# Moving the compressed entries' causal mask from TensorE to VectorE, both heads at once, and reordering the start of an attention kernel

## The chip, the core and the metric

The kernel runs on one core of a Trainium2 chip. The metric is device time in microseconds; a kernel's time is the median of its runs. The core has a matrix engine (TensorE, PE in the profile; its weight loads are PEld), VectorE (DVE), ScalarE (ACT), GpSimd (POOL) and SyncE (SP), which here only issues DMAs. PE writes to PSUM; the other data lies in SBUF.

## What is computed

Four sequences of 1024 tokens with 512 features go through one block. With `xn` the layer-normalized input, the output is `x + attn(xn) + ffn(xn)`, where `ffn` is one product with operands rounded to 8-bit floats. The attention has 16 heads of 128 and two branches that share queries:

```python
q = apply_rope(rmsnorm(q, qn_w), pos)
entries = jnp.einsum('bcr,bcrh->bch', w_cmp, hidden_states.reshape(Bq, C, RATIO, HID))
ck = apply_rope(rmsnorm(entries @ Wk + bk, kn_w), block_ends)
sc = jnp.einsum('bhsd,bcd->bhsc', q, ck) * scale
sc = jnp.where(causal, sc, NEG)
tv, ti = jax.lax.top_k(sc, TOPK)
...
sl = jnp.einsum('bhcqd,bhckd->bhcqk', qc, kw) * scale
sl = jnp.where(mask[None, None], sl, NEG)
pl = jax.nn.softmax(sl, axis=-1)
...
merged = (ctx_sparse + ctx_local) * 0.5
```

Four tokens make one compressed entry. A token weighs the 8 best entries whose block has ended, with a softmax over those 8, and separately the tokens of its own and the previous window of 128. Both contexts are averaged and go through `Wo`.

## The kernel before

The work is cut into chunks of 128 tokens (8 per sequence, 32 in all) and each chunk into 8 units of two heads, so there are 256 units. All weights stay in SBUF. One Python loop (lines 835 to 904) writes the program out; each engine runs its instructions in that order. Its step `s` mixes stages of several units, so that a unit is spread over six steps:

- `queries` of unit s+3 (L478): queries and window keys of two heads, four products of 512 columns. In chunk 0 a bias product (L486) follows; later chunks have the bias folded into the weights by `fold_first_row` (L269), which chunk 0 runs once per unit.
- `squares` (L318, ScalarE) and `spread` (GpSimd) of s+3 give the RMS norm; `normalize` of s+2 (L506, VectorE) applies it and starts `rotate`: a GpSimd product (L332), a VectorE product (L333), and behind a `yield` two VectorE combinations (L335, L336), run later by `end_rotation`.
- Keys and queries must be transposed. In chunk 0 PE does it (`turn_keys_here`, L534) and `keep_keys` copies them out (L540 ScalarE, L541 VectorE). Later `turn_keys` of s+2 transposes 32x32 blocks on VectorE (L556, L559), stores them to DRAM (L564) and `fetch_keys` loads them back in the other order (L574), all from SP's queue.
- `scores` of s, for each head: previous window (L616), own window (L623), entries (L626), and a product of an identity and the mask in bf16 (L627) that adds the causal mask to the last 32 entries. Each head has a PSUM tile `sc` of one bank.
- `weigh` of s, for each head: add the window's mask and take the smallest negated score (L649), the 8 largest entries (L652), their negated maximum (L654), mark the 8 (L655, into `taken`), and two exponentials on ScalarE (L656, L664).
- `settle` of s, for each head: multiply by the marks and sum (L671), floor and reciprocal of the two sums (L680, L681), scale the entries (L682); `settle_window` scales the window on ScalarE (L687).
- `turn` of s transposes blocks of the probabilities (L705), stores them (L713), and `fetch` loads them (L747). In chunk 0 and the last unit `turn_here` (L728) uses PE, and `keep_turned` copies (L736) one head on ScalarE and one on VectorE.
- `values_of` of s+1 (L581) and `keep_values` (L593); `values` of s-1 (L764) makes the context, `keep_context` of s-2 (L779) copies it and `to_output` of s-2 (L797) multiplies by `Wo`.

Two generators run beside this by `steps()`: `chunk_prep` (layer norm, entries, their keys and values) and `chunk_eight` (the 8-bit product). For chunk 0 `until` runs `chunk_prep` up to named steps before the loop and in its first three steps. The PSUM tag `pp` has two buffers, shared in turn by xp, yp, tq, vp, tp and others.

At the start, loads are issued from SP's and ScalarE's queues in program order. A queue's issue can wait until an earlier load has landed: eight DMA semaphores are used in turn, and an issue that reuses one waits for its former load.

Of the kernel before, what the change touches and what calls it, by code (L numbers as in the profile page):

```python
# [38 lines left out]
def kernel(  # L39
# [93 lines left out]
    load_x(0, "norm")  # L133
    load_wqk(0, nc.sync)
    load_x(1, "norm")
    load_angles(0)

    wkv_sb = const.tile([P, KK, 2 * D + 1], F32, name="wkv_sb")
    nc.sync.dma_start(wkv_sb[:, :, 0:D], Wk.rearrange("(k p) n -> p k n", p=P))
    nc.sync.dma_start(wkv_sb[:, :, D : 2 * D], Wv.rearrange("(k p) n -> p k n", p=P))  # L140
    load_wlv(0, nc.sync)
    load_wqk(1, nc.sync)
    load_angles(1)
    load_wlv(1, nc.sync)
    load_wqk(2, nc.sync)
    load_wlv(2, nc.sync)


    with nc.allow_non_contiguous_dma(reason="512 words once"):
        nc.scalar.dma_start(  # L150
            wkv_sb[:, :, 2 * D : 2 * D + 1], Wcmp.rearrange("(k p) o -> p k o", p=P)
        )
    bias_f = work.tile([P, 1024], F32, tag="probT", name="bias_f", bufs=1)[0:BLK, 0:512]
    nc.vector.memset(bias_f, 0.0)
    nc.scalar.dma_start(bias_f[0:NU, 0:256], bq.rearrange("(u n) -> u n", u=NU))
    nc.scalar.dma_start(bias_f[0:NU, 256:512], blk.rearrange("(u n) -> u n", u=NU))
    bkv_sb = const.tile([NE, 2 * D], F32, name="bkv_sb")
    nc.scalar.dma_start(bkv_sb[:, 0:D], bk.partition_broadcast(NE))
    nc.scalar.dma_start(bkv_sb[:, D : 2 * D], bv.partition_broadcast(NE))
    norm_w = const.tile([P, 2, D], F32, name="norm_w")  # L160
    nc.scalar.dma_start(norm_w[:, 0, :], qn_w.partition_broadcast(P))
    nc.scalar.dma_start(norm_w[:, 1, :], kn_w.partition_broadcast(P))
    blv_n = work.tile([P, 2, P], F32, tag="cT", name="blv_n", bufs=1)[0:NH, 0, :]
    nc.scalar.dma_start(blv_n, blv.rearrange("(h d) -> h d", h=NH))
    bcmp_sb = const.tile([P, 1], F32, name="bcmp_sb")
    nc.scalar.dma_start(bcmp_sb, bcmp.partition_broadcast(P))
    scales = const.tile([P, 2], F32, name="scales")
    nc.scalar.dma_start(scales[:, 0:1], scale.partition_broadcast(P))
    nc.scalar.dma_start(scales[:, 1:2], scale1.partition_broadcast(P))


    nhalf = const.tile([P, 4], F32, name="nhalf")
# [7 lines left out]
    ident_b = const.tile([P, P], BF16, name="ident_b")  # L180
    inv = const.tile([P, 1], F32, name="inv")
    bias_b = const.tile([P, 512], BF16, name="bias_b")
    nc.vector.memset(bias_b, 0.0)
# [136 lines left out]
    def rotate(th, cs, nh, a, name):  # L320

        p = th.shape[0]
        a = a.rearrange("p (h t f) -> p h t f", h=nh, t=2)
        bb = work.tile([p, nh, 2, HALF], F32, tag=f"ropeb{nh}", name=f"rb_{name}", bufs=1)
        x12 = th[:, :, 0:ROPE].rearrange("p h (t f) -> p h t f", t=2)

        def wide(v):
            return v.unsqueeze(1).unsqueeze(1).to_broadcast([p, nh, 2, HALF])  # L330

        nc.gpsimd.tensor_tensor(bb, x12, wide(cs[:, HALF:ROPE]), ALU.mult)  # L332
        nc.vector.tensor_tensor(a, x12, wide(cs[:, 0:HALF]), ALU.mult)  # L333
        yield
        nc.vector.tensor_tensor(x12[:, :, 0, :], a[:, :, 0, :], bb[:, :, 1, :], ALU.subtract)  # L335
        nc.vector.tensor_tensor(x12[:, :, 1, :], a[:, :, 1, :], bb[:, :, 0, :], ALU.add)  # L336
# [5 lines left out]
    def chunk_prep(t):  # L342
# [14 lines left out]
        if c == 0:  # L357
            nc.gpsimd.memset(cv, 0.0)
        yield "B0"

        off = work.tile([P, 2], F32, tag="off", name=f"off_{t}")
        nc.gpsimd.tensor_scalar(off[:, 0:1], st[:, 6:7], -1.0, None, ALU.mult)
        nc.scalar.activation(
            xt, xt, AF.Identity, bias=off[:, 0:1], scale=1.0, accum_out=off[:, 1:2]
        )
        nc.gpsimd.tensor_scalar(off[:, 1:2], off[:, 1:2], 1.0 / HID, None, ALU.mult)
        yield "A1"
        xn = scratch(f"xn_{t}")
        nc.vector.tensor_scalar(xn, xt, off[:, 1:2], r, ALU.subtract, ALU.mult)
# [149 lines left out]

    def end_rotation(n):  # L520
        for _ in units[n].pop("rotation"):
            pass
# [13 lines left out]
    def keep_keys(n):  # L536
        w = units[n]
        tq = w.pop("tq").rearrange("p (t g a i) -> p t g a i", t=2, g=2, a=NB)
        qT, lkT = key_tiles(n)
        nc.scalar.copy(qT.rearrange("p a (i g) -> p g a i", g=2), tq[:, 0])  # L540
        nc.vector.tensor_copy(lkT.rearrange("p a (g i) -> p g a i", g=2), tq[:, 1])  # L541
# [55 lines left out]
    heads = {}  # L597
# [9 lines left out]
    def scores(n, h):  # L607
        t, _ = place(n)
        c, m, loc, spa = columns(n)
        w = units[n]  # L610
        qT, lkT = w["qT"], w["lkT"]
        ckT, _ = entries[t // NCH]
        sc = psum.tile([P, 512], F32, tag="sc", name=f"sc_{n}_{h}")
        q = qT[:, :, h]
        if c:
            nc.tensor.matmul(  # L616
                blocks(sc[:, 0:P]),
                q,
                units[n - NU]["lkT"][:, :, ds(h * BLK, BLK)],
                start=True,  # L620
                stop=True,
            )
        nc.tensor.matmul(  # L623
            blocks(sc[:, P : 2 * P]), q, lkT[:, :, ds(h * BLK, BLK)], start=True, stop=True
        )
        nc.tensor.matmul(sc[:, spa], q, ckT[:, 0:m], start=True, stop=False)  # L626
        nc.tensor.matmul(  # L627
            sc[:, ds(2 * P + m - NE, NE)],
            ident_b,
            mask_b[:, 2 * P : 2 * P + NE],  # L630
            start=False,
            stop=True,
        )
        heads[n, h] = {"sc": sc}

    def weigh(n, h):
        c, m, loc, spa = columns(n)
        w = heads[n, h]
        sc = w.pop("sc")
        top = work.tile([P, 8], F32, tag="top", name=f"top_{n}_{h}")  # L640
        neg = work.tile([P, 2], F32, tag="neg", name=f"neg_{n}_{h}")
        tot = work.tile([P, 2], F32, tag="tot", name=f"tot_{n}_{h}", bufs=3)
        taken = work.tile([P, 2 * P], BF16, tag="taken", name=f"taken_{n}_{h}")
        prob = probs[h]
        if n % (NU * NCH) == 0:

            nc.gpsimd.memset(prob[:, 2 * P + NE : 4 * P], 0.0)

        nc.vector.tensor_tensor_reduce(  # L649
            sc[:, loc], sc[:, loc], mask_b[:, loc], -1.0, TAKEN, ALU.add, ALU.min, neg[:, 0:1]  # L650
        )
        nc.vector.max(top, sc[:, spa])  # L652

        nc.vector.tensor_scalar(neg[:, 1:2], top[:, 0:1], -1.0, 1e29, ALU.mult, ALU.min)  # L654
        nc.vector.match_replace(taken[:, 0:m], top, sc[:, spa], TAKEN)  # L655
        nc.scalar.activation(  # L656
            prob[:, loc],
            sc[:, loc],
            AF.Exp,
            bias=neg[:, 0:1],  # L660
            scale=-1.0,
            accum_out=tot[:, 0:1],
        )
        nc.scalar.activation(prob[:, spa], sc[:, spa], AF.Exp, bias=neg[:, 1:2])  # L664
        w.update(tot=tot, taken=taken, prob=prob)

    def settle(n, h):
        c, m, loc, spa = columns(n)
        w = heads[n, h]
        tot, taken, prob = w["tot"], w["taken"], w["prob"]  # L670
        nc.vector.scalar_tensor_tensor(  # L671
            prob[:, spa],
            taken[:, 0:m],
            TAKEN_FROM,
            prob[:, spa],
            ALU.is_ge,
            ALU.mult,
            accum_out=tot[:, 1:2],
        )
        nc.vector.tensor_scalar(tot, tot, 1e-9, None, ALU.max)  # L680
        nc.vector.reciprocal(tot, tot)  # L681
        nc.vector.tensor_scalar(prob[:, spa], prob[:, spa], tot[:, 1:2], None, ALU.mult)  # L682

    def settle_window(n, h):
        _, _, loc, _ = columns(n)
        prob, tot = heads[n, h]["prob"], heads[n, h]["tot"]
        nc.scalar.mul(prob[:, loc], prob[:, loc], tot[:, 0:1])  # L687
# [10 lines left out]
    def turn(n):  # L698
# [4 lines left out]
        for h in range(2):  # L703
            prob = heads.pop((n, h))["prob"]
# [11 lines left out]
    def turn_here(n):  # L716
# [4 lines left out]
        for h in range(2):  # L721
            prob = heads.pop((n, h))["prob"]
# [8 lines left out]
    def keep_turned(n):  # L731
# [3 lines left out]
        for h, tp in enumerate(w.pop("tp")):  # L735
            (nc.vector.tensor_copy if h else nc.scalar.copy)(  # L736
# [89 lines left out]

    first, rounding = chunk_prep(0), round_w2()
    until(first, "A1")
    nc.vector.tensor_copy(ident_b, ident)
# [5 lines left out]
    for s in range(-3, NN + 2):  # L835
# [13 lines left out]
        for_unit(s, (weigh, 0), (weigh, 1))  # L849
        for_unit(s + 3, (queries,))  # L850
        if s + 1 < NU:
            for_unit(s + 1, (turn_keys_here,))
        for_unit(s, (settle, 0), (settle, 1))
        for_unit(s, (settle_window, 0), (settle_window, 1))
        for_unit(s + 2, (normalize,))
        if by_dma(s):
            turn(s)
        if s < 0:
            until(first, ("B3", "B4", "B6")[s + 3])
# [7 lines left out]
        if s + 2 >= NU:  # L867
            for_unit(s + 2, (turn_keys,))
        if s == -1:
            until(first, "B7")  # L870
        for_unit(s + 1, (values_of,))
# [15 lines left out]
        if s < NU:  # L887

            if s == -1:
# [61 lines left out]
```

## Time and profile before

| | us |
|---|---|
| median of 3 runs (2798.2 to 2800.68) | 2800.16 |
| the profiled execution | 2798.32 |
| its span | 2796.6 |
| to the first scores | 44.2 |
| chunk 0's eight units | 113.6 |
| the other 248 units | 2616.4 |
| from the last unit's scores to the end | 22.4 |

The mean granted TensorE clock over the span is 0.994; over the first 44.2 us it is 0.92, over chunk 0 0.89, and in between up to the last unit 1.00.

In a row of the profile, `L627 PE MATMUL sc<-mask_b,ident_b` is line, engine, operation and output from inputs; `xN` counts instructions, "mean ns" is the mean of one, and "idle before" the time its engine stood idle just ahead of them, with what ended it. In rows of a time line the first number is the start, the second the time up to the end of the last of the merged instructions. A product in fp32 appears as two instructions. In rows of waits the three numbers are the sum, the count and the longest.

### The profile page before, as it was taken

What the parts mean: (1) busy time and instruction counts of PE and PEld (TensorE: products, weight loads), DVE (VectorE), ACT (ScalarE), POOL (GpSimd) and SP (SyncE); (2) the same over time, 40 slices, a digit from 0 to 9 for tenths busy, and PEclk for the clock granted to TensorE, in tenths of its full rate; (3) what the DMA queues carried; (4) which work ended last, traced back from release to release, by engine and by line L of the source; (5) the groups of instructions that cost most, each with busy time, mean ns of one, the idle gap of its engine ahead of it and who ended that gap; (6) DMA issues with size and microseconds to landing.
All of it is one profiled execution on the core that took longest, in us unless ns stands there. A gap on an engine that the chain in (4) does not pass through costs nothing.

```text
span 2796.6 us, 48466 instructions
## 1 busy us (share of the span) xinstructions
PE 2735.4 (98%) x12721; PEld 1856.4 (66%) x12721; DVE 2263.3 (81%) x9171; ACT 1345.1 (48%) x5170; POOL 842.6 (30%) x1225
## 2 busy tenths in 40 slices
PE   5799999999999999999999999999999999999998
PEld 3566666676666666666666666666666666666765
DVE  4687888888877788888888787888888878888886
ACT  2345544445455554444445455454444545544443
POOL 2333332233332333322233322333223333222321
PEclk9899999999999999999999999999999999999999
DMA  6345445555544545555554454555555444455554
GB/s 203 98 119 139 136 136 155 154 154 154 146 125 139 139 141 141 154 152 152 153 142 134 132 140 138 152 155 145 153 149 143 129 139 139 136 152 161 145 150 125
DMA packets 623187, 401.96 MB, mean 144 GB/s; under 512 B 307152, under 2 KB 576320, under 8 KB 622912
## 3 DMA queue, kind: packets, MB, share of 16 engines
q1 hardware_dynamic: 610688, 385.29, 50.2%
q10 hardware_dynamic: 12224, 13.56, 1.6%
q8 instruction: 104, 1.70, 0.3%
q14 instruction: 171, 1.40, 0.2%
HBM read 214.64 MB, written 184.03 MB: 143 GB/s over the span
## 4 chain that ended last, share of the span: by engine, by line
PE 92%; DVE 2%; DMA 1%; issue 0%; SPq 0%; ACT 0%; POOL 0%; DVEq 0%; ACTq 0%; POOLq 0%
PE qp L478 30%; PE op L797 15%; PE vp L581 15%; PE cp L764 14%; PE sc L626 5%; PE sc L616 4%; PE sc L623 4%; PE yp L386 2%; PE fp L458 1%; PE ep L416 1%; PE xp L373 0%; DVE wqk L269 0%; DMA probT<-pr 0%; PE sc L627 0%; DVE th L506 0%
## 5 line engine op out<-in xcount | busy, mean ns | idle before, releaser
L478 PE MATMUL qp<-wqk,xnT 128*128 128x512 f32 x2048 | 944.7, 604 | 2.8 <-issue 2.1
L332 POOL TENSOR_TENSOR rb<-th,cs 128x256 f32<-128x256 f32 x256 | 248.1, 969 | 1673.7 <-DVE th L506 1673.7
L478 PEld LDWEIGHTS qp<-wqk,xnT 128*128 128x128 f32 x2048 | 370.3, 191 | 382.9 <-issue 371.7
L581 PEld LDWEIGHTS vp<-wlv,xnT 128*128 128x128 f32 x2048 | 393.0, 192 | 181.6 <-issue 115.8
L581 PE MATMUL vp<-wlv,xnT 128*128 128x256 f32 x2048 | 490.9, 383 | 17.9 <-DVE lkT L541 13.6
L656 ACT ACTIVATE prob<-sc,neg 128x256 f32<-128x256 f32 (+1 forms) x512 | 235.6, 460 | 550.9 <-DVE taken L655 540.4
L797 PE MATMUL op<-wo,cT 128*128 128x512 f32 x1024 | 488.0, 599 | 0.5 <-ACT cT L779 0.5
L649 DVE CUSTOM_DVE_ANT_0 sc<-sc,mask_b 128x256 f32<-128x256 f32 (+1 forms) x512 | 208.0, 406 | 279.8 <-PE sc L627 279.6
L593 ACT COPY lv<-vp 128x256 f32<-128x256 f32 x256 | 95.2, 372 | 471.6 <-PE cp L764 412.7
L687 ACT ACTIVATE prob<-prob,tot 128x256 f32<-128x256 f32 (+1 forms) x512 | 252.4, 493 | 129.1 <-DVE tot L681 127.8
L797 PEld LDWEIGHTS op<-wo,cT 128*128 128x128 f32 x1024 | 186.4, 190 | 189.4 <-issue 129.2
L764 PE MATMUL cp<-probT,lv 128*128 128x128 f32 x1920 | 300.7, 277 | 6.3 <-DMA probT<-pr 5.7
L318 ACT ACTIVATE junk<-qp 128x128 bf16<-128x128 f32 x1024 | 279.7, 273 | 33.1 <-PE qp L478 5.0
L506 DVE SCALAR_TENSOR_TENSOR th<-qp,r,norm_w 128x128 f32<-128x128 f32 x1024 | 286.8, 343 | 5.7 <-ACT junk L318 3.2
L764 PEld LDWEIGHTS cp<-probT,lv 128*128 128x128 f32 x1920 | 275.5, 193 | 23.4 <-issue 10.3
L705 DVE STREAM_TRANSPOSE probB<-prob 128x512 f32<-128x512 f32 (+2 forms) x494 | 281.9, 608 | 0.0
L313 POOL TENSOR_TENSOR r<-r,nhalf 128x4 f32<-128x4 f32 x256 | 260.5, 1018 | 21.3
L764 PE MATMUL cp<-probT,cv 128*128 128x128 f32 x1536 | 257.1, 277 | 0.0
L626 PE MATMUL sc<-ckT,qT 128*128 128x96 f32 (+7 forms) x1024 | 226.3, 303 | 0.0
L764 PEld LDWEIGHTS cp<-probT,cv 128*128 128x128 f32 x1536 | 214.8, 194 | 0.0
L623 PE MATMUL sc<-lkT,qT 128*128 128x128 f32 x1024 | 207.9, 285 | 0.0
L779 ACT ACTIVATE cT<-cp,blvT 128x128 f32<-128x128 f32 x512 | 160.0, 364 | 92.7 <-PE cp L764 83.4
(130 smaller groups left out, 3802.1 us busy)
## 6 DMA issues: line engine op xcount, KB each, us to landing
pr<-probB SPq DMA_DIRECT2D x127, 512.0 KB, 2.6
probT<-pr SPq DMA_DIRECT2D x508, 128.0 KB, 2.9
qk<-thb SPq DMA_DIRECT2D x992, 64.0 KB, 1.8
pr<-probB SPq DMA_DIRECT2D x96, 384.0 KB, 2.3
probT<-pr SPq DMA_DIRECT2D x384, 96.0 KB, 2.4
qT<-qk SPq DMA_DIRECT2D x248, 128.0 KB, 2.9
lkT<-qk SPq DMA_DIRECT2D x248, 128.0 KB, 2.8
x_norm<-_attn_hidden_states_dram SPq DMA_DIRECT2D x32, 256.0 KB, 3.0
```

Source lines behind the costliest of these rows:

```text
L313: nc.gpsimd.tensor_tensor(r, r, nhalf[: ss.shape[0], 0:n], ALU.pow)
L318: nc.scalar.activation(junk[: src.shape[0]], src, AF.Square, accum_out=acc)
L332: nc.gpsimd.tensor_tensor(bb, x12, wide(cs[:, HALF:ROPE]), ALU.mult)
L478: nc.tensor.matmul(qp, xnT[:, k if k or not t else KK, :], wqk_sb[u][:, k, :], start=(k == 0), stop=(t > 0 and k == KK - 1),)
L506: nc.vector.scalar_tensor_tensor(th[:, i, :], qp[:, ts(i, D)], r[:, i : i + 1], norm_w[:, i // 2, :], ALU.mult, ALU.mult,)
L581: nc.tensor.matmul(vp[:, 0:256], xnT[:, k, :], wlv_sb[u][:, k, :], start=(k == 0), stop=(k == KK - 1),)
L623: nc.tensor.matmul(blocks(sc[:, P : 2 * P]), q, lkT[:, :, ds(h * BLK, BLK)], start=True, stop=True)
L626: nc.tensor.matmul(sc[:, spa], q, ckT[:, 0:m], start=True, stop=False)
L687: nc.scalar.mul(prob[:, loc], prob[:, loc], tot[:, 0:1])
L705: nc.vector.transpose(pb[:, :, ds(h * g, g), :], prob[:, parts[0] * P : (parts[-1] + 1) * P].rearrange("p (g b i) -> p b g i", b=NB, i=BLK),)
L764: nc.tensor.matmul(blocks(cp[:, h, :]), v, probT[:, :, h * len(parts) + i - parts[0], :], start=(i == parts[0]), stop=(i == parts[-1]),)
L797: nc.tensor.matmul(op, cT[:, h, :], wo_sb[u][:, h, :], start=(u == 0 and h == 0), stop=(u == NU - 1 and h == 1),)
```

## The change

The last 32 entries' mask is added by one VectorE instruction for both heads, in PSUM, and L627 is gone. `sc` becomes one tile of two banks with one buffer. `weigh`, `settle` and `settle_window` handle both heads in one call; all marking stands ahead of the exponentials, and negation, floor and reciprocal are done once for both heads. `normalize` of s+2 stands between `weigh` and `settle`, and `rotate` has one more `yield`, so that its VectorE product follows `settle_window`.

```diff
+        if not h:
+            w["sc"] = psum.tile([P, 2, 512], F32, tag="sc", name=f"sc_{n}", bufs=1)
+        sc = w["sc"][:, h, :]
...
-        nc.tensor.matmul(sc[:, spa], q, ckT[:, 0:m], start=True, stop=False)
-        nc.tensor.matmul(
-            sc[:, ds(2 * P + m - NE, NE)],
-            ident_b,
-            mask_b[:, 2 * P : 2 * P + NE],
-            start=False,
-            stop=True,
-        )
+        nc.tensor.matmul(sc[:, spa], q, ckT[:, 0:m], start=True, stop=True)
...
+        last = sc[:, :, ds(2 * P + m - NE, NE)]
+        nc.vector.tensor_tensor(
+            last,
+            last,
+            mask_b[:, 2 * P : 2 * P + NE].unsqueeze(1).to_broadcast([P, 2, NE]),
+            ALU.add,
+        )
+        for h in range(2):
+            nc.vector.max(top[:, h, :], sc[:, h, spa])
+            if h:
+
+                nc.vector.tensor_scalar(
+                    neg[:, :, 1], top[:, :, 0], -1.0, 1e29, ALU.mult, ALU.min
+                )
+            nc.vector.match_replace(taken[:, h, 0:m], top[:, h, :], sc[:, h, spa], TAKEN)
...
         nc.gpsimd.tensor_tensor(bb, x12, wide(cs[:, HALF:ROPE]), ALU.mult)
+        yield
         nc.vector.tensor_tensor(a, x12, wide(cs[:, 0:HALF]), ALU.mult)
...
-        for_unit(s, (weigh, 0), (weigh, 1))
+        for_unit(s, (weigh,))
+        if 0 <= s < NU - 1:
+            for_unit(s + 1, (turn_keys_here,))
         for_unit(s + 3, (queries,))
-        if s + 1 < NU:
+        if s < 0:
             for_unit(s + 1, (turn_keys_here,))
-        for_unit(s, (settle, 0), (settle, 1))
-        for_unit(s, (settle_window, 0), (settle_window, 1))
+            until(first, ("B3", "A6", "B6")[s + 3])
         for_unit(s + 2, (normalize,))
+        for_unit(s, (settle,))
+        for_unit(s, (settle_window,))
+        for_unit(s + 2, (go_on_rotating,))
```

In chunk 0 the copies L541 and the second of L736 move from VectorE to ScalarE. Chunk 0's layer norm subtracts the mean of the statistics on VectorE, without ScalarE's second pass (L363) and the two GpSimd instructions around it. Twelve bf16 products of a zero tile run on PE ahead of everything. Units' key transposes stand ahead of the next queries. The values of unit 0 stand ahead of the entries' keys. The loads are issued in a new order: the biases first on ScalarE's queue, then `Wcmp`, the norm weights and the small biases; on SP's queue `Wk` and `Wv` directly behind the first query weights, then the second ones, the rotation's angles, the second chunk's rows, the third query weights, and the value weights last. The loads of `blv` and the two scales move to the end of step -2.

```diff
-            (nc.vector.tensor_copy if h else nc.scalar.copy)(
+            nc.scalar.copy(
...
+        xn = None
+        if t:
...
+        else:
+            xn = scratch(f"xn_{t}")
+            nc.vector.tensor_scalar(xn, xt, st[:, 6:7], r, ALU.subtract, ALU.mult)
...
+    warm = pp("warm")
+    for _ in range(12):
+        nc.tensor.matmul(warm, bias_b[:, 0:P], bias_b, start=True, stop=True)
```

## The prediction

> **What bounds the kernel now.** I read the page's busy times and chain first, then the groups of instructions by line, then time lines of TensorE.
>
> ```profile
> PE 2735.4 (98%) x12721; PEld 1856.4 (66%) x12721; DVE 2263.3 (81%) x9171; ACT 1345.1 (48%) x5170; POOL 842.6 (30%) x1225
> PE 92%; DVE 2%; DMA 1%; issue 0%; SPq 0%; ACT 0%; POOL 0%; DVEq 0%; ACTq 0%; POOLq 0%
> ```
>
> A busy PE alone proves little, since its ends are modelled, but the chain agrees: 92% of it is PE. Cut into stages (busy time by stretches), the span is 44.2 us to the first scores, 113.6 for chunk 0 (8 units, 14.2 us each, PE busy 88.1), 2616.4 for the other 248 units (PE busy 2610.1) and 22.4 at the end. In the long stage PE never rests: a unit takes 9.40 us in the first chunk of a sequence and 11.1 to 11.3 in the last, while VectorE is busy 7.6 and 9.6 of it. So what leaves PE's stream counts in the long stage, and what shortens chains counts in the first 158 us.
>
> **The mask leaves TensorE.** The time line of PE in a unit of a sequence's first chunk (32 entries):
>
> ```profile
> 1503.76 0.40 PE L623 MATMUL sc<-lkT,qT 128*128 128x128 f32 x2
> 1503.99 0.32 PE L626 MATMUL sc<-ckT,qT 128*128 128x32 f32 x2
> 1504.14 0.18 PE L627 MATMUL sc<-mask_b,ident_b 128*128 128x32 bf16 x1
> 1504.17 0.48 PE L623 MATMUL sc<-lkT,qT 128*128 128x128 f32 x2
> 1504.49 0.32 PE L626 MATMUL sc<-ckT,qT 128*128 128x32 f32 x2
> ```
>
> [...] The pair on L623 takes 0.23 us to the next start in head 0, but 0.32 behind a mask product (L627), which itself takes 0.03. In nanoseconds of the trace: 28 to the next start, and then 199 instead of 117 between the two halves of the following product (512 instead of 429 where it is a query product). So a mask product costs 28 + 83 = 0.11 us. The Trainium skill, "TensorE: Matmul & The Clock Gate", section "Wait — 56ns, not 53.3ns?", puts the floor of a small matmul at about 25 ns start to start, and its "Step-by-step: what each phase is for" has the next weights load while the running matmul streams. By that rule 496 products (248 units, two heads) are worth 496 x 0.028 = 14 us; by the row 496 x 0.11 = 54.6 us. The row speaks of 253 queries and 224 scores behind a mask product alike, so I take 54.6: a product this short cannot cover the load behind it. The 0.18 of the busy column (89 us) overlaps and is the upper end.
>
> **VectorE gets the mask.** Added per unit: one in-place sum of 128x2x32 in PSUM. The trace of before has no such row; near ones are 32x64 (L333, 0.21) and 128x128 (L335, 0.27), both from SBUF; I take 0.25, bounds 0.15 and 0.45. Removed per unit, by handling both heads in one instruction: one negation (0.08 to the next start), one L680 and one L681 (0.20 each): 0.48. That is 0.23 less work. It is hidden under PE, but its order moves.
>
> (a) The first masking step now waits for both heads' scores (its one wait covers the common tile). With 192 entries scores end 1.78 us after their start and not 0.99, so this begins 0.8 later; with 32 entries about 0.2 to 0.3.
> (b) The exponentials wait until both heads are marked, 2.9 us after masking begins (192 entries: 2 x 0.53, 0.27, 2 x 0.40, 2 x 0.33, 0.08) instead of 1.33. Queued behind the waiting ScalarE instruction are the window's scaling, the squares and chunk 0's key copies. VectorE has normalization (4 x 0.28 = 1.15) in between, so its first marked product (L671) finds its exponentials done, its second waits 0.3.
> (c) The rotation's GpSimd product (L332) now starts when normalization ends, beside L671, where before it stood beside its own VectorE half and the transposes.
>
> ```profile
> 64.11 1.27 POOL L291 TENSOR_TENSOR wo<-wo 128x512 f32<-128x512 f32 x1
> 64.30 1.12 DVE L671 SCALAR_TENSOR_TENSOR prob<-taken,prob 128x32 f32<-128x32 bf16 x1
> 66.05 0.18 DVE L671 SCALAR_TENSOR_TENSOR prob<-taken,prob 128x32 f32<-128x32 bf16 x1
> ```
>
> An L671 that meets GpSimd ends when GpSimd does, 1.12 us instead of 0.18. The skill's "SBUF — State Buffer", section "SBUF: two separate sides", states it as a rule: a VectorE instruction with two SBUF inputs and a GpSimd one exclude each other for the whole instruction. This speaks against the change. The row of L332 (0.97 us, of which about 0.38 is the wait for L333, which began 0.04 earlier) leaves 0.6 of its own. With the rule the second L671 starts 1.0 after normalization; without it 0.65 to 0.7. So (b) and (c) cost 0.6 together by the rule, 0.3 without; against the 0.23 saved, marking to transposes takes about 8.1 us instead of 7.5. I take the rule. Bounds per unit for VectorE: -0.2 and +1.1.
>
> **Who waits for that.** VectorE idles about 1.1 us per unit for scores (279.6 us in all), so its throughput holds. The deadline is the round trip of the probabilities through DRAM:
>
> ```profile
> 1251.62 1.83 SPq L747 DMA_DIRECT2D probT<-pr  x4
> 1256.46 0.28 PE L764 MATMUL cp<-probT,lv 128*128 128x128 f32 x1
> PE cp L764 <- DMA probT<-pr: 5.7, 4, 2.2
> ```
>
> These four loads stand on SP behind the key stores (L564), which wait for VectorE's last transposes (L559). From issue to landing they take 2.9 us (page), so this unit's landed at 1256.2, 0.27 before their product. Over all chunks the trace gives, from last landing to first product, a median of 0.54 us for unit 6 of a chunk, 1.04 for unit 5 and over 2 for the others. The product comes two units later, so the margin loses 2 x 0.22. Unit 5 gains: its VectorE waited 1.2 us for a GpSimd product (L335 on rb_e, 37.6 us in all) that is out of the way now. Unit 6 starts 0.25 later and ends 0.55 later: 0.54 - 0.44 - 0.80 = -0.7 us. PE waits 0.7 in each of 31 chunks, 22 us; unit 0's keys, with a median margin of 1.0, add a little. I take 25; bounds 0 and 50.
>
> **The first 158 us.** Chunk 0's LayerNorm now uses the mean directly: no ScalarE pass (0.72 + 0.18), no two GpSimd steps, and no wait for ScalarE's queue of DMA issues, which held it to 9.27:
>
> ```profile
> 9.27 1.28 ACT L363 ACT_TABLE_LOAD   x1 [9.27 <-DMA blv_n<-in_L_attn_blv_dram]
> 14.14 6.52 PE L478 MATMUL qp<-wqk,xnT 128*128 128x512 f32 x8 [0.68 <-ACT xnT L376]
> 22.46 3.60 PE L478 MATMUL qp<-wqk,xnT 128*128 128x512 f32 x8
> ```
>
> The hidden rows' statistics are ready at 5.73; the normalized rows then at 6.4 (11.71 + 0.59 before), transposes to 7.5. ScalarE has eight issues and its table load ahead, to about 6.6; the copy ends at 8.1, as both first weights land (8.1 before). The first queries start at 8.2, not 14.14. At the half clock of before they take 6.52, at the full one 3.5; the twelve warm-up products may grant it. It decides little, since the bias product waits for VectorE's bias chain (4.0 us after the norm weights, which land about 8.5): 12.5 to 12.9. Entries 1.9 and second queries 4.0 give 18.7 (26.3 before); third queries wait for the first buffer, 21.3 (28.4); then keys, values before the entries' keys, scores at about 30 instead of 44.2. The loads are the same bytes in another order; what moves back (scales, the third weights, blv) has over 5 us. I take 13 gained, bounds 4 and 16. Of the moved issues, blv's and the scales' three (0.4 each) now stand in ScalarE's queue ahead of the third queries' squares.
>
> In chunk 0 the loop was ScalarE squares, copy, VectorE copy (L541), transposes, products, both copies (L736), fold (L269, 2.28), marking, settling: 12.2 and 11.9 us in units 5 and 6. With both copies on ScalarE (0.38 each; it is busy 39.4 of 113.6), the fold no longer waits for PE. PE's own work, about 10.2, then sets plain units; the first four keep their quantization and DMA issues. 1.5 to 2 us in eight units: 14 gained, bounds 5 and 22. Ident's bf16 copy (0.2) and the earlier key transposes change nothing: the queries behind them have slack.
>
> **Sum**, against the profiled execution (2798.3, of which 2796.6 is span; 1.8 under the median 2800.2): -54.6 + 25 - 13 - 14 = -56.6, span 2740.0, execution 2741.7; at the median 2743.6, say 2743.
>
> **Rivals.** *Covers hold*: the lock does not bite and unit 6 keeps its margin; for it, unit 5's gain precedes it; against, the median is 0.54. 2800.2 - 54.6 - 27 = 2719. *The product goes, its load stays*: PE gains 14, 0.06 a unit; unit 6 then lacks 0.54 - 0.12 - 0.80 = 0.4, 12 us in 31 chunks: 2800.2 - 14 + 12 - 27 = 2771. The 83 ns stand behind no other product in the trace, which speaks against it. *The start gains nothing*, if the loads' new order holds it: 2800.2 - 54.6 + 25 = 2771. *VectorE becomes the bound* (slower): place, marking to transposes, by late exponentials and the lock. Its idle time less the shorter unit is 1.1 - 0.22 = 0.9 per unit; beyond it each 0.1 costs 25 us. The 82 us gained are lost from 1.2 us more per unit; at 1.3, 2800.2 - 82 + 99 = 2817. For it: the idle time is zero in units 6 and 7 already; against: my bound is 1.1.
>
> **Chances.** Forecast 0.52; covers hold 0.20; load stays 0.10; start gains nothing 0.06; VectorE bound 0.12. All but the last are faster. A difference within 0.2%, 5.6 us, cannot be told from none and has 0.02, taken from the edges. The range 2705 to 2790 leaves out most of the last case and a start at its best bound.
>
> **What would show it.** the entries' score (L626) followed by its neighbour as closely as any other product of its width; unit length 0.2 less where PE is unbroken; waits of the context product for probT in units 6, some 20 us in all; a longer second L671 beside the rotation's GpSimd product; first queries near 8 us and first scores near 30. Wrong if waits for probT appear in most units, or if the score products' spacing does not shrink.

## The result, and the profile after

The changed kernel takes 2783.28 us (median of 4 runs, 2782.66 to 2785.53) beside 2799.18 (2797.98 to 2800.68) for the kernel before: a ratio of 0.9942, with an interval of 0.993 to 0.9955. It is faster by 16 us, not by 57. The profiled execution took 2785.53, its span 2783.8.

The page of the changed kernel, busy times and chain:

```profile
PE 2701.9 (97%) x12221; PEld 1822.8 (65%) x12221; DVE 2223.0 (80%) x8641; ACT 1298.3 (47%) x5185; POOL 804.6 (29%) x1223
PE 2%; DVE 1%; ACT 0%; DMA 0%; SPq 0%; issue 0%; POOL 0%; ACTq 0%; DVEq 0%; POOLq 0%
```

PE is busy 33.5 us less, but the span shrank by only 12.8. The chain, 92% PE before, now reaches back over some 3% of the span only, so it cannot say what bounds the kernel. The stages say more:

| us | before | after | predicted difference | measured |
|---|---|---|---|---|
| to the first scores | 44.25 | 34.99 | -13 | -9.3 |
| chunk 0's eight units | 113.5 | 92.8 | -14 | -20.7 |
| the other 248 units | 2616.4 | 2631.1 | -29.6 | +14.7 |
| from the last unit's scores to the end | 22.4 | 24.9 | 0 | +2.5 |

The early part came out as forecast in its sum (30.0 for 27), though not in its two terms. The long stage was to shrink by 54.6 less 25 and grew instead. Three rows of waits (sum, count, longest) of the changed kernel answer to the prediction's row for probT (5.7, 4, 2.2) and to its two other concerns:

```profile
DVE prob L696 <- ACT prob L688: 96.4, 255, 1.1
DVE kv L337 <- POOL rb_e L333: 58.5, 32, 1.8
PE cp L793 <- DMA probT<-pr: 47.6, 54, 2.2
```

VectorE's wait for the exponentials is 0.38 per unit (forecast 0.3). The wait on rb_e, which was to vanish, grew from 37.6 to 58.5. PE's wait for the probabilities is 47.6, and its count 54 is not 31: the trace has it 29 times for the probabilities of a unit 5 and 21 times for those of a unit 6. Against a unit of unbroken PE, the long stage lost 35.5 us in the periods of units 6 (where the probabilities of unit 5 are needed) and 22.2 in those of units 7 (those of unit 6).

The mask itself, in PE's time line of a changed unit with 32 entries (start, duration):

```profile
1462.22 0.40 PE L635 MATMUL sc<-lkT,qT 128*128 128x128 f32 x2
1462.45 0.32 PE L638 MATMUL sc<-ckT,qT 128*128 128x32 f32 x2
1462.61 0.48 PE L635 MATMUL sc<-lkT,qT 128*128 128x128 f32 x2
1462.92 0.32 PE L638 MATMUL sc<-ckT,qT 128*128 128x32 f32 x2
```

The mask products are gone, yet head 1's L635 still takes 0.31 us to the next start, against 0.23 for head 0's: the 83 ns that the prediction put down to the mask product stand here behind the entries' product of 32 columns. Only where that product is wide does the delay go. Behind a mask product the two halves of the next one lay 198 ns apart; in the changed kernel they lie 199, 171, 144 and 118 ns apart behind an entries' product of 32, 64, 96 and 128 columns, and 109 behind a wider one. The median of unit 3, which never waits, shows it:

| entries | 32 | 64 | 96 | 128 | 160 | 192 | 224 | 256 |
|---|---|---|---|---|---|---|---|---|
| before, us | 8.77 | 9.74 | 9.80 | 9.85 | 10.38 | 10.49 | 10.60 | 10.70 |
| after, us | 8.71 | 9.63 | 9.63 | 9.63 | 10.15 | 10.26 | 10.37 | 10.47 |

By units, 24 x 0.06 + 32 x (0.11 + 0.17 + 0.22 + 4 x 0.23) = 47 us saved, where 54.6 were forecast.

What happened to unit 5 is seen in one of them, with 96 entries. The kernel before, from GpSimd's product of the rotation to the key stores:

```profile
1653.17 0.97 POOL L332 TENSOR_TENSOR rb<-th,cs 128x256 f32<-128x256 f32 x1 [8.20 <-DVE th L506]
...
1653.19 0.28 ACT L318 ACTIVATE junk<-qp 128x128 bf16<-128x128 f32 x1
...
1654.49 0.54 POOL L313 TENSOR_TENSOR er<-er,nhalf 32x1 f32<-32x1 f32 x1
...
1655.11 0.35 POOL L312 TENSOR_SCALAR r<-ss 128x4 f32<-128x4 f32 x1
...
1655.55 1.01 POOL L313 TENSOR_TENSOR r<-r,nhalf 128x4 f32<-128x4 f32 x1
1656.53 0.31 POOL L332 TENSOR_TENSOR rb_e<-kv,cse 32x64 f32<-32x64 f32 x1
1656.88 0.18 DVE L335 TENSOR_TENSOR kv<-ra_e,rb_e 32x32 f32<-32x32 f32 x1 [1.23 <-POOL rb_e L332]
...
1658.40 0.80 SPq L564 DMA_DIRECT2D qk<-thb  x2
```

The same unit in the changed kernel:

```profile
1629.18 0.73 POOL L333 TENSOR_TENSOR rb<-th,cs 128x256 f32<-128x256 f32 x1 [5.25 <-DVE th L514]
...
1630.54 0.91 ACT L716 ACTIVATE prob<-prob,tot 128x256 f32<-128x256 f32 x2 [0.89 <-DVE tot L706]
...
1632.28 0.28 ACT L319 ACTIVATE junk<-qp 128x128 bf16<-128x128 f32 x1
...
1633.93 0.19 POOL L313 TENSOR_SCALAR r<-ss 128x4 f32<-128x4 f32 x1 [0.84 <-ACT junk L319]
...
1634.21 1.01 POOL L314 TENSOR_TENSOR r<-r,nhalf 128x4 f32<-128x4 f32 x1
1635.20 0.31 POOL L333 TENSOR_TENSOR rb_e<-kv,cse 32x64 f32<-32x64 f32 x1
1635.54 0.18 DVE L337 TENSOR_TENSOR kv<-ra_e,rb_e 32x32 f32<-32x32 f32 x1 [1.83 <-POOL rb_e L333]
...
1637.06 0.81 SPq L575 DMA_DIRECT2D qk<-thb  x2
```

The unit's scores began at 1646.94 before and at 1623.94 after. So the squares of unit s+3 start 6.25 us into the unit before, and 8.34 after. In both kernels rb_e, the rotation product of the chunk's new entries, is queued on GpSimd directly behind the RMS steps (r, 1.3 us). Before, GpSimd was busy without a break from the rotation's product on, and r followed at once. Now that product is long done, and r waits 0.84 us for the last of the four squares. VectorE waits for rb_e, and behind it stand the last rotation sums and the key transposes. On SP's queue the probabilities' loads stand behind the key stores.

### The profile page after: what moved, and what is told of

It reads as the page before. It is cut to its first block, busy times and chain, and to the rows that moved or that the text cites. A ratio compares the mean times of both kernels' runs of the same rounds, so it can differ in the third digit from the quotient of the medians.

```text
span 2783.8 us, 47080 instructions
## 1 busy us (share of the span) xinstructions
PE 2701.9 (97%) x12221; PEld 1822.8 (65%) x12221; DVE 2223.0 (80%) x8641; ACT 1298.3 (47%) x5185; POOL 804.6 (29%) x1223
## 5 line engine op out<-in xcount | busy, mean ns | idle before, releaser
L486 PE MATMUL qp<-wqk,xnT 128*128 128x512 f32 x2048 | 930.2, 597 | 4.7 <-ACT xnT L384 2.9
L486 PEld LDWEIGHTS qp<-wqk,xnT 128*128 128x128 f32 x2048 | 378.1, 191 | 376.9 <-issue 372.4
L333 POOL TENSOR_TENSOR rb<-th,cs 128x256 f32<-128x256 f32 x256 | 203.7, 796 | 1068.3 <-DVE th L514 1068.3
L793 PE MATMUL cp<-probT,lv 128*128 128x128 f32 x1920 | 303.6, 278 | 50.6 <-DMA probT<-pr 47.6
L716 ACT ACTIVATE prob<-prob,tot 128x256 f32<-128x256 f32 (+1 forms) x512 | 225.5, 487 | 256.9 <-DVE tot L706 254.2
L696 DVE SCALAR_TENSOR_TENSOR prob<-taken,prob 128x128 f32<-128x128 bf16 (+7 forms) x512 | 185.3, 362 | 97.1 <-ACT prob L688 96.4
L635 PE MATMUL sc<-lkT,qT 128*128 128x128 f32 x1024 | 207.9, 285 | 1.3 <-DVE ckT L455 0.9
L313 POOL TENSOR_SCALAR r<-ss 128x4 f32<-128x4 f32 x256 | 57.9, 226 | 490.5 <-ACT junk L319 485.2
```

The costliest lines, as they stand in the source:

```text
L486: nc.tensor.matmul(qp, xnT[:, k if k or not t else KK, :], wqk_sb[u][:, k, :], start=(k == 0), stop=(t > 0 and k == KK - 1),)
L716: nc.scalar.mul(probs[h][:, loc], probs[h][:, loc], tot[:, h, 0:1])
L793: nc.tensor.matmul(blocks(cp[:, h, :]), v, probT[:, :, h * len(parts) + i - parts[0], :], start=(i == parts[0]), stop=(i == parts[-1]),)
```

## The experiments

Theory A is that chain: late exponentials, late squares, late r, late rb_e, late key stores, late probabilities. Theory B is a VectorE path that is too long in every unit, theory C SP's own queue. All runs are compared with runs of the kernel before on the same chip (medians 2799.0 to 2800.2); "lost" is what the long stage's units take beyond an unbroken unit of their kind without the mask.

**1. GpSimd's RMS steps behind the entries' rotation.**

```diff
-        for_unit(s + 3, (squares, (0, 1, 2, 3)), (spread,))
+        for_unit(s + 3, (squares, (0, 1, 2, 3)))
...
         steps()
+        for_unit(s + 3, (spread,))
```

> The changed kernel with one move: the GpSimd steps of spread for unit s+3 (L313, L314) stand behind the second steps() instead of ahead of it. Theory A (in unit 5 of a chunk the late exponentials make the window's scaling and so ScalarE's squares late; spread waits for the squares and takes 1.2 us, and the entries' rotation rb_e is queued behind it on GpSimd, so that VectorE waits up to 1.8 us, key stores and with them the probabilities' loads go late): rb_e starts some 1.7 us earlier in unit 5, its wait falls from 58 us to under 15, PE's waits for probT in units 5 and 6 fall from 47.6 us to under 10, and the time from 2783 to about 2740. Theory B (marking to transposes is too long in every unit): unit 5 gains, unit 6 keeps its 0.9 us, 2760. Theory C (the loads' own queue and its semaphores hold them): no change, 2783.

Measured 2743.1 us, ratio 0.9795 (0.9778 to 0.9811): 40 us faster than the changed kernel, by one moved line. Its rows:

```profile
DVE kv L337 <- POOL rb_e L333: 8.3, 32, 1.7
PE cp L793 <- DMA probT<-pr: 14.8, 18, 2.4
```

The wait on rb_e is gone. The same unit 5 has this order on GpSimd, from 1599.94 on:

```profile
1609.53 0.35 POOL L333 TENSOR_TENSOR rb_e<-kv,cse 32x64 f32<-32x64 f32 x1 [0.45 <-DVE kv L445]
1609.91 0.18 DVE L337 TENSOR_TENSOR kv<-ra_e,rb_e 32x32 f32<-32x32 f32 x1 [0.21 <-POOL rb_e L333]
1609.96 0.30 POOL L313 TENSOR_SCALAR r<-ss 128x4 f32<-128x4 f32 x1
...
1611.43 1.79 SPq L575 DMA_DIRECT2D qk<-thb  x4
```

Key stores are issued 11.5 us into the unit, before 11.5 and in the changed kernel 13.1. Lost time in the periods of units 6 went from 35.5 to nothing, in those of units 7 from 22.2 to 15.1. Theory A holds for unit 5, and C falls, since SP's queue was left as it was. PE's wait, 14.8 us, is above the expected 10: something of its own is left in unit 6.

**2. The probabilities' loads on ScalarE's queue.**

```diff
-            nc.sync.dma_start(
+            nc.scalar.dma_start(
                 probT[ds(b * BLK, BLK)].rearrange("j a g i -> j a (g i)"), turned[b]
...
         for_unit(s + 1, (keep_values,))
+        if by_dma(s):
+            fetch(s)
```

> The changed kernel with the four loads of probT issued from ScalarE's queue, behind keep_values, instead of from SP's queue behind the key stores. Theory A and B alike (what costs is that these loads stand behind key stores that wait for VectorE's last transposes): they are issued some 11 us into a unit and not up to 15, PE's waits for probT go from 47.6 to under 5 us, 2783 - 50 = 2733. Rival D (the deadline isn't what costs, or ScalarE pays for it): four issues of about 0.45 us each, 1.8 us per unit, push contexts and exponentials back, VectorE gets its marks later, and the time stays at 2775 to 2800.

Measured 2791.2, ratio 0.9969 (0.9957 to 0.9981): rival D. PE no longer waits for probT directly, but ScalarE does, and the contexts behind it come late:

```profile
ACT cT L808 <- DMA qk<-thb: 430.2, 102, 6.4
ACT cT L808 <- DMA probT<-pr: 276.4, 77, 6.2
PE op L826 <- ACT cT L808: 55.4, 45, 3.8
```

The first two rows are the idle time of ScalarE ahead of L808, where the issues stand: up to 6.4 us. Of their 706.7 us some 299 are the issues themselves (about 0.45 each, 1.8 per unit, as rival D has it); the rest is waiting for older transfers to land. A new wait took the place of the old one. This run does not speak on the cause, only on the cure.

**3. The mask products left out of the kernel before.** (The lines of L627 are deleted, so this kernel leaves out the causal mask of the last 32 entries.)

> The kernel before with the mask products simply left out; nothing takes their place, so the entries' causal mask of the last 32 entries is left out of the computation. By the prediction's 0.11 us for each of 496 products: 2800 - 55 = 2745. By the changed kernel's unbroken units (0.058 us shorter per unit at 32 entries, 0.11 at 64, 0.17 at 96, 0.22 from 128 on): about 46 less, 2754. If the load stays exposed behind it: 14 less, 2786. In each, shorter units also bring unit 6's probT closer to its product, which may give back up to 10.

Measured 2765.9, ratio 0.9877 (0.9862 to 0.9892), 33.5 less and between the expectations. The long stage is 36.8 shorter. Its undisturbed units have the lengths of the changed kernel (8.71 at 32 entries, 10.26 at 192), so a mask product's worth depends on the product in front of it, as in the table above. The rest of the 47 is lost again in the periods of units 7 (10.1 us): even with nothing added to VectorE, shorter PE units eat the cover.

**4 and 5. The steady part alone, the early part alone.** Run 4 is the kernel before with the new weighing, settling and order; run 5 is the kernel before with the loads, the first products and chunk 0's copies.

> The kernel before with only the part that runs in every unit: the mask on VectorE for both heads, weighing and settling of both heads in one, normalization ahead of settling, the rotation's VectorE half behind it. Loads, first products and chunk 0's copies stay as before. By the stages of the changed kernel (the early stages gave 30 us, the long stage and the end cost 17): about 2815, slower than before by 0.5%. Rival: early part and steady part are not additive (chunk 0 gains from the steady part too, with fewer VectorE instructions): 2800 or less.

> The kernel before with only the early part: new order of loads, warm-up products, chunk 0's direct layer norm, its copies on ScalarE, earlier key transposes and values. Mask, weighing and settling stay as before. By the prediction: 27 less, 2772. By the changed kernel's stages: 9 to the first scores, 21 in chunk 0: 2769. By the difference between the changed kernel and its steady part alone: 45 less, 2754, which would mean that chunk 0 gains from the early part what the steady part costs there.

Measured 2828.4 (1.0102, 1.0087 to 1.0117; expected 2815, or 2800 and less) and 2766.4 (0.988, 0.9866 to 0.9895; expected 2754 to 2772). So the part that runs in every unit made the kernel slower by 29 us, and the early part made it faster by 33; together they give -16. The long stage of run 4 is 15.4 longer than before, as in the changed kernel (14.7); that of run 5 is unchanged (2616.5). The 12 us that don't add up lie mostly in chunk 0: the steady part alone costs 8.3 there (121.8 us for 113.5), which the early part takes away again (92.8 for both, 92.6 for the early part). Which of chunk 0's steps pays the 8.3 was not tried.

**6. Key transposes ahead of the second `steps()`.**

```diff
-        steps()
         for_unit(s + 2, (end_rotation,))
         if s + 2 >= NU:
             for_unit(s + 2, (turn_keys,))
+        steps()
```

> The changed kernel with the second steps() moved behind turn_keys; spread stays ahead of it, so rb_e still waits behind the RMS steps on GpSimd and VectorE still waits for rb_e in unit 5, but no longer ahead of the key transposes. Theory A (that wait costs only because key stores and the probabilities' loads stand behind it): waits on rb_e stay at 40 to 58 us, PE's waits for probT fall from 47.6 to under 20, 2783 - 35 = 2748. If the wait on rb_e costs by VectorE's own time, which is full in units 5 to 7: no change, 2783.

Measured 2727.3, ratio 0.9747 (0.9731 to 0.9763). Its rows are the sharpest test of the chain:

```profile
DVE kv L337 <- POOL rb_e L333: 46.3, 32, 1.8
PE cp L793 <- DMA probT<-pr: 5.7, 8, 2.2
```

VectorE still waits for rb_e, 1.8 at the longest, but key stores and probabilities no longer stand behind that wait, and PE's waits are back at 5.7. What the wait cost came from its place in the order, not from VectorE's time. The gain, 56 us for 35 expected, is not unit 5's alone: the second `steps()` also issues the second step of the 8-bit product in unit 6, and lost time in the periods of units 7 fell too, from 22.2 to 4.6 us (runs 8 and 9 take the two apart).

**7. Control: the move of run 1 in the kernel before.**

> The kernel before with the same move as in the first run (GpSimd's RMS steps for unit s+3 behind the second steps()). A control: if the order of these GpSimd steps costs only together with the change, PE has waits for probT of 5.7 us to lose here and the time stays at 2795 to 2800. If the move is a gain of its own, whatever the change: about 2760.

Measured 2799.0, ratio 0.9997 (0.9987 to 1.0006). Its wait on rb_e fell from 37.6 to 6.8 us, and nothing was gained: before the change this wait was covered. Run 1's gain belongs to the change's lateness.

**8 and 9. The 8-bit product's steps behind the key transposes,** alone (8) and together with run 1's move (9).

```diff
         if s + 2 >= NU:
             for_unit(s + 2, (turn_keys,))
+        if eight:
+            next(eight, None)
+            next(eight, None)
```

> The changed kernel with only both steps of the 8-bit product's generator moved behind turn_keys; spread stays where it is. Theory A, by units: the wait in unit 6's period (probabilities of unit 5, 35 us in all) is due to rb_e and stays; the one in unit 7's period (probabilities of unit 6, 22 us) is due to quantization and the stretched rotation sum ahead of unit 6's key stores, and goes: 2783 - 20 = 2763. If unit 6 is late only because unit 5 was: no change, 2783.

> The changed kernel with the GpSimd move of the first run, and both steps of the 8-bit product's generator (three VectorE instructions and GpSimd sums over 128x512 in unit 6) moved behind turn_keys. Theory A says that what is left of the waits for probT (14.8 us in the first run, u7 losing 0.5 us per chunk) comes from unit 6's key stores behind these: 1.3 us of quantization and a rotation sum stretched from 0.27 to 1.36 us beside GpSimd's sum. Then the waits go, some 12 us: 2743 - 12 = 2731. Rival: the next unit's masking stands behind them instead and VectorE falls behind by as much: 2743 or a little more.

Run 8 measured 2757.0 (0.985, 0.9837 to 0.9864), run 9 2724.4 (0.9731, 0.9716 to 0.9745). Lost time in the periods of units 6 and 7 was 35.5 and 22.2 in the changed kernel; in run 8 it is 34.2 and 0.6, in run 9 1.7 and 0.1. The two waits have two causes, and each move takes away its own. Unit 6's is seen in the changed kernel, just ahead of its key stores:

```profile
1644.47 0.43 DVE L289 TENSOR_SCALAR qm_x<-qm_x 128x512 f32<-128x512 f32 x1
...
1645.04 1.28 POOL L290 TENSOR_TENSOR qv_x<-qv_x,qm_x 128x512 f32<-128x512 f32 x1 [3.74 <-DVE ckT L455]
1645.11 1.36 DVE L338 TENSOR_TENSOR th<-thb,rb 128x128 f32<-128x128 f32 x1
```

Three quantizing instructions (0.43 each) go ahead of the rotation's sums, and the second sum takes 1.36 us beside GpSimd's, where in unit 5 it takes 0.27. In the kernel before it takes 1.36 there too, with the cover to bear it.

**10. The mask on VectorE with nothing reordered,** on top of the early part:

```diff
+        last = sc[:, ds(2 * P + m - NE, NE)]
+        nc.vector.tensor_tensor(last, last, mask_b[:, 2 * P : 2 * P + NE], ALU.add)
         nc.vector.max(top, sc[:, spa])
```

> The early part alone with one thing added: the entries' mask by VectorE, for each head in its own instruction between the window's mask and the 8 largest. Separate score tiles, exponentials behind each head's marking, settling and normalization stay as before, so nothing is reordered. Two VectorE instructions of about 0.2 us more per unit, none saved. Theory A (the reordering, by late squares, is what made unit 5 late): the wait on rb_e stays near 40 us, unit 5 keeps its cover, unit 6 loses 0.23 x 2 by shorter units and 0.4 x 3 by VectorE, waits about 1.1 in each of 31 chunks: 2766 - 46 + 34 = 2754. If VectorE's addition itself, not the order, is what costs: waits for probT in units 5 and 6 as in the changed kernel, 2770 to 2785.

Measured 2755.5, ratio 0.9844 (0.9831 to 0.9858). Two plain instructions more per unit, and it beats the changed kernel by 28 us.

```profile
DVE kv L337 <- POOL rb_e L334: 39.8, 32, 1.7
PE cp L767 <- DMA probT<-pr: 30.4, 28, 3.3
```

Here the waits are unit 6's alone (32.8 us lost in the periods of units 7, 1.0 in those of units 6). It is not the mask's place on VectorE that makes unit 5 late, but the new order. In unit 6 the two added instructions do cost: 32.8 us lost, where run 3, without any mask, lost 10.1.

**11. Settling ahead of normalization again,** in the changed kernel:

```diff
-        for_unit(s + 2, (normalize,))
         for_unit(s, (settle,))
         for_unit(s, (settle_window,))
+        for_unit(s + 2, (normalize,))
```

> The changed kernel with one part undone: settle and settle_window stand ahead of normalize again; marking of both heads stays ahead of the exponentials. It asks which part of the reordering makes ScalarE's squares late (2.1 us in unit 5). If it is normalization in between (1.03 us on VectorE): squares start 1 us earlier, rb_e's wait falls from 58 to about 30 us, and the time to about 2755. If it is the marking of both heads ahead of the exponentials: the first settling must now wait for its exponential with nothing in between, about 0.9 us more idle VectorE per unit in waits on L688, squares come only some 0.4 us earlier, rb_e's wait stays above 40, key stores go 0.6 later in every unit, and the time rises to about 2800.

Measured 2844.5, ratio 1.0171 (1.0152 to 1.019), beyond either expectation but of the second kind:

```profile
DVE prob L696 <- ACT prob L688: 345.9, 508, 1.9
PE cp L793 <- DMA probT<-pr: 90.4, 70, 3.3
```

The squares start no earlier (8.25 for 8.34 us in unit 5 with 96 entries). Normalization in between is therefore not what makes them late. It is a needed cover: without it VectorE waits 1.0 us more per unit for exponentials that begin only when both heads are marked. What is left is the common score tile, the marking of both heads ahead of the exponentials, and the common reciprocal that both window scalings now wait for (L716 behind L706 above). No run tried these singly; in the table below masking starts 0.69 us later, the last exponential ends 1.59 later and the squares start 2.09 later.

**12. Both moves that free the key stores** (6 and 8).

> The changed kernel with the second steps() and both steps of the 8-bit product behind turn_keys, spread where it is. Both causes of late key stores are gone; what is left of lost time in the long stage was 11 us with the first move alone and 8 with the spread and 8-bit moves. Expected: 2720, the fastest of these; if VectorE only carries its lateness into the next unit, 2727.

Measured 2722.1 us (2719.6 to 2723.7), ratio 0.9722 (0.9709 to 0.9736), the fastest here, though run 9 cannot be told from it. PE waits 4.5 us for probabilities in all, and the long stage takes 48.0 less than before: what the mask's removal is worth (47) is now had.

The chain in numbers, medians of unit 5 in the chunks with 96 entries, in us from the start of its scores:

| | before | after | run 10 | run 11 | run 1 | run 6 |
|---|---|---|---|---|---|---|
| masking starts | 0.90 | 1.59 | 0.88 | 1.59 | 1.59 | 1.59 |
| last exponential ends | 4.12 | 5.71 | 4.57 | 5.71 | 5.71 | 5.71 |
| squares of s+3 start | 6.25 | 8.34 | 6.70 | 8.25 | 8.34 | 8.34 |
| rb_e starts | 9.59 | 11.26 | 10.06 | 11.38 | 9.59 | 11.25 |
| key transposes end | 11.43 | 13.09 | 11.89 | 13.22 | 11.47 | 9.47 |
| first load of probT is issued | 13.34 | 15.01 | 13.81 | 15.14 | 13.38 | 11.90 |
| last one has landed | 17.20 | 18.81 | 17.70 | 19.08 | 17.24 | 15.78 |
| their product starts | 18.63 | 18.94 | 18.29 | 19.22 | 18.29 | 18.29 |

## Why the prediction was wrong

The sign was right, but by the early part alone: the long stage, from which the mask went, went the other way. The wait that was forecast, for unit 6's probabilities, came. The early total was right by luck in part: the start gave 3.7 us less than forecast, chunk 0 6.7 more. The failed step is the term "+25", the waits for probT, and in it the sentence that unit 5 gains because the wait on rb_e "is out of the way now". The long stage saved about 47 us in PE's stream and still grew by 14.7, so this term was about 62, of which 58 stand in the periods of units 6 and 7.

- **Unit 5.** The prediction freed rb_e from the rotation's product ahead of it on GpSimd, which did move away. It overlooked r, which stood directly in front of rb_e all along, and what r would then wait for. In (b) it named the squares as queued behind the waiting exponentials, and followed nobody who waits for squares. They came 2.1 us later, r began to wait for them, the wait on rb_e grew from 1.2 to 1.8 us at its longest, and unit 5 became the first late unit (run 1, run 6).
- **Unit 6.** It inherits a part of this: its masking starts 3.39 us into the unit and not 1.56 (96 entries). It was forecast to lack 0.7 us and lost 22.2 / 31 = 0.7, but beside unit 5's 35.5 / 31 = 1.1, not in place of it. That the two 0.7 agree is luck: with unit 5 repaired in run 1 it lost 15, and with the 8-bit steps moved in run 8 almost nothing; the forecast named neither. The term's upper bound of 50 was too low. In run 10, where unit 5 does keep its cover, unit 6 alone lost 33. That run 1 measures the forecast's total, 2743, is partly chance: the mask gave 8 us less than forecast, chunk 0 more.
- **The mask, 54.6.** 47 by undisturbed units. The row was read for the pair behind a mask product only, and the sentence that the delay stands "behind no other product in the trace" was wrong. In the kernel before, the 31 transposes of the entries' keys, 32 columns wide and without a mask, are followed by an output product whose first two halves lie 533 ns apart and not 429:

```profile
1242.25 0.24 PE L445 MATMUL cp<-ident,kv 32*128 32x32 f32 x1
1242.42 1.98 PE L797 MATMUL op<-wo,cT 128*128 128x512 f32 x4
1244.24 1.89 PE L581 MATMUL vp<-wlv,xnT 128*128 128x256 f32 x8
```

  The four instructions on L797 take 1.82 us to the next start here, and 1.71 or 1.72 in the two neighbouring units. (The same 533 stand behind the 31 sums of L416, which are 257 columns wide with weights of 32; what sets them there was not tried.) At 32 entries the rival "the product goes, its load stays" is right (0.03 us for each product), from 128 on the prediction is (0.11). By the floor of about 25 ns start to start that the Trainium skill states for a small product ("TensorE: Matmul & The Clock Gate", section "Wait — 56ns, not 53.3ns?"), one would estimate about 0.025 us for each throughout; this trace agrees only where the product in front is as short as the mask's.
- **VectorE's own path.** Forecast 0.6 longer from marking to transposes, and later by 0.2 to 0.8 at the start. Measured in unit 4 with 96 entries: masking starts 0.69 later, and from there to the end of the key transposes it takes 8.44 us, before 8.42. So in that unit the late start was the whole cost, and theory B falls. The lock (c) was over-sized: the second L696 takes 0.34 instead of 0.25 beside the rotation's product, not 0.3 more. The skill's rule in "SBUF — State Buffer", section "SBUF: two separate sides", that of such a pair the one that starts second is blocked until the first is done, is seen in part. With 96 entries the second L696 starts about 0.23 us ahead of the end of the rotation's product and ends 0.11 behind it; the long sum above (1.36 for 0.27) ends 0.15 behind GpSimd's. So the price is about what is left of the GpSimd instruction, and less: by the rule a whole L696 or sum, 0.25 or 0.27, would follow.
- **The start.** First queries began at 9.95, not 8.2. ScalarE's table load was to end at 6.6, with the copy behind it, and shows what held it:

```profile
8.02 1.28 ACT L384 ACT_TABLE_LOAD   x1 [8.02 <-DMA bcmp_sb<-in_L_attn_bcmp_dram]
9.31 0.59 ACT L384 COPY xnT<-xp 128x512 f32<-128x512 f32 x1
9.95 5.16 PE L486 MATMUL qp<-wqk,xnT 128*128 128x512 f32 x8 [2.86 <-ACT xnT L384]
```

  The issues ahead of it on ScalarE's queue ended at 8.0. Nor did the warm-up products carry the full clock into these queries: the granted clock was 0.71 from 9.9 to 15.2 us, their halves lie 0.85 us apart until 12.7 and 0.43 from 13.2 on, and they took 5.16 us, not 3.5. Kernels with the same early part reached their first scores anywhere from 32.3 to 35.0 us. Chunk 0 gave 20.7 for a forecast of 14; the early part alone gives 21.0 there (run 5), and which of its steps gives the rest was not tried.
- **VectorE as the bound** did not come: it is busy 80% of the span, 81% before. The end grew by 2.5 us, which no step had; it did so in run 3 as well (+2.4), where nothing was reordered, and its cause stays open.

## What to carry to other kernels

When a step is moved back in time, follow every instruction that is queued behind it on its own engine to whoever waits for it, and then what is queued behind that waiter: here the chain went through ScalarE, GpSimd, VectorE and SP's queue before it reached the matmul. A wait costs by what stands behind it in order, so ask first whether urgent work (stores that start a round trip) can go ahead of it; moving one line brought 40 us, and running the rest behind the urgent stores made a kernel 2.8% faster than before. And when a short instruction is charged with a delay, look for the same delay behind other short instructions before you count on its going.

## What the runs showed of the hardware

- A short bf16 matmul between fp32 products has no fixed price. Behind a 32-column product it cost 0.03 us, behind one of 128 columns or more 0.11. The delay behind it (83 ns) also stands behind a 32-column fp32 product, and shrinks as that product gets wider: the next halves lie 199, 171, 144 and 118 ns apart behind 32, 64, 96 and 128 columns.
- Issuing four loads per unit from ScalarE's queue held that engine for hundreds of microseconds in all (430.2 and 276.4 in run 2): some 299 by the issues themselves, 0.45 each, the rest by waiting for older transfers.
- A VectorE sum in SBUF that started 0.07 us behind a GpSimd sum of 1.28 us lasted 1.36 us instead of 0.27; an L696 that started 0.5 us into a GpSimd product of 0.73 took 0.34 instead of 0.25. Both ended 0.11 to 0.15 us behind GpSimd's.
